# A graph attention layer: the clamp of the message weights in an instruction of its own, with its result in PSUM

## The chip, the core and the metric

One core of a Trainium2 chip runs the whole kernel in one launch. The metric is the device time in microseconds. The kernel before takes 2019.45 us, the median of three runs (2014.69 to 2023.74). Five engines run side by side, each through its own list of instructions in order: TensorE (PE, with its weight loads PEld), VectorE (DVE), ScalarE (ACT), GpSimd (POOL) and SyncE (SP). They wait for each other through semaphores.

## The reference, cut to what matters

A graph has 6250 nodes of 64 features and 206250 edges, sorted by destination. Each edge makes four scores, one for each head of 16 features, and the exponential of a clipped score weighs the value of the edge's source node. The sums go to the destination nodes, the input is added, and a layer norm over 64 features ends it.

```python
Qh = (x @ Wq.T + bq).reshape(n, H, D)          # n 6250, H 4, D 16
Kh = (x @ Wk.T + bk).reshape(n, H, D)
Vh = (x @ Wv.T + bv).reshape(n, H, D)
Ee = (edge_attr @ We.T + be).reshape(-1, H, D) # 206250 edges
score = (Kh[src] * Qh[dst] * (1.0 / np.sqrt(D)) * Ee).sum(-1)
score = jnp.exp(jnp.clip(score, -5.0, 5.0))
msg = Vh[src] * score[..., None]
wV = jax.ops.segment_sum(msg, dst, num_segments=n)
x = _layernorm(x + wV.reshape(n, H * D), axis=-1)
```

## The kernel before, in words

**Tiles and groups.** The edges are cut into 1612 tiles of 128 edges, one edge to a partition, and eight tiles make a group `g`; there are 202 groups. Two groups make a step `s`, apart from the last eight groups, which are steps of their own. After a stage that makes a table of keys and values in HBM (`kv_tab`) and a table of queries, one Python loop over `g` (L1014) writes out the instructions of all groups by hand. No scheduler reorders them: the order of the calls in that loop is the order on each engine.

**What one turn of the loop does.** POOL fetches the keys and values of the sources, 128 rows to an indirect DMA (`gather_kv`, L296), into one of five tiles `kv` in SBUF; most groups need eight of these DMAs, some need six because PE makes the rows of their last two tiles itself. PE turns the edge features and the queries of a group into `room` and `qq` in PSUM; ACT adds a bias (`eb`, L755), DVE multiplies the two (`term`, L769) and PE transposes the result into `qe` (L775), one of two PSUM banks that alternate by group. From there the group goes through DVE and ACT:

- `products` (L806, L808), DVE: `prod` is the keys of `kv` in SBUF times `qe` in PSUM, and `score` its sum over each head, 128 x 32.
- `weigh` (L813, L815), ACT: the upper clip and the exponential, into `weight`, a tile of 128 x 32 in SBUF.
- `message` (L830), DVE: one SCALAR_TENSOR_TENSOR instruction takes the larger of `weight` and the constant `LEAST` (e to the power of -5, the lower clip) and multiplies it with the values of `kv`. Both of its tensors lie in SBUF. Its output overwrites `qe`, except in the last steps, where it goes into `kv`.
- `keep` (L844), ACT, copies that to `msg` rounded, and `take` (L850), DVE, stores what the rounding left. PE adds the messages of a step up by one-hot matrices into `room` in the next turn (`sums`).

**What shares these engines.** PE also makes rows of `kv` by one-hot products, in batches `m` over pieces of the node table: DVE writes one-hot matrices (`hots`, L696, named `hot`, or `thin` where ACT widens them at L707), PE multiplies them (`picks`, into the two banks `pick`), DVE selects from the two banks (`picked`, L722 and L723, into `x`), and PE makes the rows from that (`picked_kv`, into `qq`). DVE also adds the sums of a step to a ring (`add`, L900 to L909), once in two turns; that work is called the ring's adds below. L744 is the line of a helper that records nearly all matmuls of the loop.

**The order around the change.** Within a turn DVE runs the products, the next group's `term`, the ring's adds if there are any, the first one-hot matrix of the next turn, `message`, the other one-hot matrices, `onehot_edges` (L792) at the end of a step, `take`, and `picked` where a batch ends.

**The bank of constants.** `still` (L660) is one PSUM bank of 128 x 512 f32 that holds what DVE reads again and again: `col` and `block2`, from which the one-hot matrices are compared, and `sum_`, into which the ring's adds reduce.

Of the kernel before, what the change touches and what calls it, by code (L numbers as in the profile page):

```python
# [14 lines left out]
OP = mybir.AluOpType  # L15
AX = mybir.AxisListType

P = 128
N = 6250
C = 64  # L20
H = 4
D = C // H
E = 206250
T = -(-E // P)
G = 8
# [31 lines left out]
LEAST = math.exp(-CLIP)  # L57
# [57 lines left out]
def place_of(g):  # L115

    s = max(s for s in range(NS) if STEPS[s][0] <= g)
    return s, (g - STEPS[s][0]) * G
# [31 lines left out]
def tile_gnn(ctx: ExitStack, tc: tile.TileContext, x, x_blocks, by_rows, xT, wT, bias, beT, weT, eT, src, src_rows,  # L150
             dst, dst_rows, out):
    nc = tc.nc
# [16 lines left out]
    def kv_of(g):  # L169

        s = max(s for s in range(NS) if STEPS[s][0] <= g)
        j = (g - STEPS[s][0]) * G
        return kvs[s % KVB][:, j:j + G, :]
# [479 lines left out]
    with tc.If(rv == 0) as branch:  # L653

        with tc.tile_pool(name="work", bufs=2) as work, \
# [3 lines left out]
            OH, OF, EB, TERM, MSG, SCORE, WEIGHT, HOT = ({} for _ in range(8))  # L659
            still = fixed.tile([P, 4 * P], F32, name="still")  # L660
# [7 lines left out]
            pa = room[:, 1, :2 * PA]  # L668
            folded = room[:, 1, 2 * PA:2 * PA + 2 * C].rearrange("p (b c) -> p b c", c=C)
            sum_ = still[:, 2 * P:2 * P + C]  # L670
            px = [fixed.tile([P, 4 * P], F32, name=f"pick{k}") for k in range(2)]
            xs = [accp.tile([P, 4 * P], F32, name=f"x{k}") for k in range(2)]
            qq = fixed.tile([P, G // 2, P], F32, name="qq")
# [143 lines left out]
            def message(g, lo, hi):  # L817
                s, k = place_of(g)
                n = hi - lo
                if s < WHOLE:  # L820
                    if k == 0:
                        MSG[s] = work.tile([P, 2 * G, 2, C], F32R, name="msg")
                        if s >= ONES:
                            MSG[s] = MSG[s].rearrange("p g i c -> p (g i c)").bitcast(BF16)[:, :G * 3 * C] \
                                .rearrange("p (g i c) -> p g i c", i=3, c=C)
                    to = qe[g % 2][:, lo:hi, :]
                else:
                    MSG[s] = kvs[(s - 2) % KVB][:, G:, :C]
                    to = MSG[s][:, lo:hi, :]
                nc.vector.scalar_tensor_tensor(  # L830
                    to.rearrange("p g (h d) -> p g h d", h=H),
                    WEIGHT.pop(g)[:, :, :, None].to_broadcast([P, n, H, D]), LEAST,
                    kv_of(g)[:, lo:hi, C:].rearrange("p g (h d) -> p g h d", h=H),
                    op0=OP.max, op1=OP.mult)

            def part_of(g, i):

# [176 lines left out]
            for g in range(NG + 1):  # L1014
# [46 lines left out]
                if now:  # L1061
                    message(g, *some_of(g)[0])
                for lo, hi in some_of(g)[1:] if now else []:
                    products(g, lo, hi)
                    weigh(g, lo, hi)
                    message(g, lo, hi)
# [255 lines left out]
```

## Time and profile before

| what | value |
|---|---|
| median of the runs | 2019.45 us |
| lowest and highest run | 2014.69 and 2023.74 us |
| the profiled execution's own time | 2023.01 us |
| its span, first to last instruction | 2021.2 us |
| granted TensorE clock, mean | 0.939 |
| PE busy | 1723.6 us, 85% of the span |
| DVE busy | 1485.3 us, 73% |
| ACT busy | 1327.1 us, 66% |
| POOL busy | 1256.9 us, 62% |

A busy time adds up an engine's instructions; what is left of the span is waiting. DVE instructions that don't wait for each other overlap by some tens of ns, so two rows can cover the same moment. A row of the timeline has start, duration, engine, line, operation and tiles, and in brackets the idle time ahead of it with what ended it. A row of the waits names who waited for whom, with total us, times and the longest. The chain of waits goes back from the last instruction, at each step to what released it; its pieces are the work that set the end.

### The profile page before, as it was taken

The page shows a single profiled execution, that of the slowest core. Times are in us where ns is not written, and L with a number is a line of the kernel's source. Part 1 is how long each engine was busy: PE and PEld are TensorE (multiplying, and loading weights), DVE is VectorE, ACT ScalarE, POOL GpSimd, SP SyncE. Part 2 cuts the span into 40 slices and gives each one's busy share as a digit, 9 for nine tenths or more (in the row PEclk, how much of TensorE's full clock was granted, in tenths as well). Part 3 has the DMA queues.
Part 4 walks back from the last instruction along what each step waited for, and adds up shares of the span by engine and source line. Part 5 has one row for each costly group of instructions (what it writes and reads, how often), then busy time and mean ns, then how long its engine had stood idle before and what let it go on. Part 6 is the DMA issues. An engine that isn't in the chain of part 4 may idle for free.

```text
span 2021.2 us, 25631 instructions
## 1 busy us (share of the span) xinstructions
PE 1723.6 (85%) x7993; PEld 1249.4 (62%) x7993; DVE 1485.3 (73%) x2650; ACT 1327.1 (66%) x2047; POOL 1256.9 (62%) x1310
## 2 busy tenths in 40 slices
PE   7468989888888888979888898888888998888995
PEld 6336666666666665656666666666666666656763
DVE  5367777777777786877777777777777777677886
ACT  3356676666666666766667766666766667576774
POOL 6566666666666666666666666666666666666441
PEclk9789999999999998999999999899999999999997
DMA  6524233233233332343333332333323333333320
GB/s 178 174 72 134 87 104 109 85 110 104 86 104 106 88 103 85 104 122 90 103 101 87 107 107 83 109 95 98 103 87 115 103 89 104 99 92 109 96 80 21
DMA packets 116116, 203.70 MB, mean 101 GB/s; under 512 B 54784, under 2 KB 56425, under 8 KB 115855
## 3 DMA queue, kind: packets, MB, share of 16 engines
q1 hardware_dynamic: 73932, 116.94, 18.7%
q0 software_dynamic: 41600, 83.97, 14.7%
q10 hardware_dynamic: 436, 1.04, 0.2%
q8 instruction: 65, 1.06, 0.2%
q14 instruction: 83, 0.68, 0.1%
HBM read 194.25 MB, written 7.59 MB: 100 GB/s over the span
## 4 chain that ended last, share of the span: by engine, by line
PE 60%; DVE 18%; issue 8%; ACT 6%; another core or an unknown queue 5%; DMA 2%; POOL 1%; SPq 0%; DVEq 0%; ACTq 0%; POOLq 0%
PE pick L744 35%; PE room L744 10%; PE qq L744 9%; PE qe L775 4%; DVE hot L696 4%; DVE score L808 2%; DVE qe L830 2%; DVE prod L806 1%; DVE term L769 1%; DVE msg L850 1%; DVE thin L696 1%; DMA kv<-kv_tab,src_i 1%; PE ps L513 1%; DVE x L722 1%
## 5 line engine op out<-in xcount | busy, mean ns | idle before, releaser
L296 POOL DMA_INDIRECT kv<-kv_tab,src_i x1260 | 1216.6, 966 | 709.4 <-issue 272.9
L744 PE MATMUL pick<-hot,parts 128*128 128x512 f32 x3900 | 1133.0, 433 | 127.6 <-DVE x L722 57.4
L744 PEld LDWEIGHTS pick<-hot,parts 128*128 128x128 f32 x3900 | 737.8, 197 | 426.7 <-issue 175.6
L696 DVE TENSOR_TENSOR hot<-from,still 128x1024 fp32r<-128x1024 bf16 x231 | 280.2, 1213 | 0.2 <-ACT from L258 0.2
L707 ACT ACTIVATE hot<-thin 128x1024 fp32r<-128x1024 bf16 x234 | 245.4, 1049 | 20.6 <-remote 16.8
L755 ACT ACTIVATE eb<-room,be_col 128x512 f32<-128x512 f32 x202 | 137.1, 678 | 150.5 <-DVE y L957 57.4
L769 DVE TENSOR_TENSOR term<-eb,qq 128x512 f32<-128x512 f32 x202 | 137.3, 679 | 125.8 <-PE qq L744 101.6
L844 ACT ACTIVATE msg<-qe 128x512 fp32r<-128x512 f32 (+1 forms) x206 | 123.2, 598 | 161.4 <-DVE qe L830 65.8
L744 PE MATMUL room<-et,we_sb 128*128 128x512 f32 x404 | 224.5, 638 | 4.3 <-ACT eb L755 3.6
L813 ACT ACTIVATE score<-score,five_p 128x32 f32<-128x32 f32 x203 | 64.2, 316 | 249.4 <-DVE score L808 161.5
L279 ACT ACTIVATE to<-to,one_p 126x1024 bf16<-126x1024 bf16 x198 | 225.7, 1140 | 0.1
L273 ACT ACTIVATE to<-kb,minus_row 126x1024 bf16<-126x1024 uint8 x198 | 225.2, 1137 | 0.0
L775 PE MATMUL qe<-ident,term 128*128 128x128 f32 x806 | 134.2, 292 | 61.1 <-DVE term L769 38.7
L775 PEld LDWEIGHTS qe<-ident,term 128*128 128x128 f32 x806 | 103.1, 150 | 114.1 <-DVE term L769 55.1
L722 DVE SCALAR_TENSOR_TENSOR x<-odd,upper,pick 128x512 f32<-128x512 int32 x77 | 57.3, 744 | 153.9 <-PE pick L744 84.8
L744 PE MATMUL qq<-w,x 128*128 128x128 f32 x1248 | 163.2, 285 | 5.3 <-issue 4.1
L806 DVE TENSOR_TENSOR prod<-kv,qe 128x512 f32<-128x512 f32 x203 | 136.9, 674 | 37.0 <-issue 13.7
L830 DVE SCALAR_TENSOR_TENSOR qe<-weight,kv 128x512 f32<-128x512 f32 x200 | 140.2, 701 | 30.2 <-ACT weight L815 20.6
L744 PEld LDWEIGHTS qq<-w,x 128*128 128x128 f32 x1248 | 153.6, 200 | 14.0 <-issue 8.1
L696 DVE TENSOR_TENSOR thin<-from,still 128x1024 bf16<-128x1024 bf16 x231 | 157.0, 680 | 0.0
L808 DVE TENSOR_REDUCE score<-prod 128x32 f32<-128x512 f32 x203 | 138.5, 682 | 7.0
L850 DVE TENSOR_TENSOR msg<-qe,msg 128x512 fp32r<-128x512 f32 x194 | 132.1, 681 | 4.3 <-ACT msg L844 2.7
(166 smaller groups left out, 1486.7 us busy)
## 6 DMA issues: line engine op xcount, KB each, us to landing
et<-in_eT SPq DMA_DIRECT2D x100, 512.0 KB
kb<-key_tab SPq DMA_DIRECT2D x101, 252.0 KB
kv<-kv_tab,src_i POOLq DMA_INDIRECT x1260
srcs<-in_src_rows SPq DMA_DIRECT2D x78, 256.0 KB
qw<-q_tab SPq DMA_DIRECT2D x202, 15.8 KB
kv_tab<-kv_sb SPq DMA_DIRECT2D x4, 640.0 KB
q_tab<-q SPq DMA_DIRECT2D x5, 480.0 KB
out<-y SPq DMA_DIRECT2D x2, 512.0 KB
```

The costliest lines, as they stand in the source:

```text
L273: nc.scalar.activation(TO[g][:, :n, :], KB.pop(g)[:, :n * P].rearrange("p (j e) -> p j e", j=n), AF.Square, bias=minus_row3[:3 * W])
L279: nc.scalar.activation(TO[g][:, :n, :], TO[g][:, :n, :], AF.Relu, bias=one_p[:3 * W], scale=-1.0)
L296: return nc.gpsimd.indirect_dma_start(out=kv_of(g)[:, j, :], out_offset=None, in_=kv_tab[:, :], in_offset=bass.IndirectOffsetOnAxis(ap=src ...
L696: nc.vector.tensor_tensor(to.rearrange("p b (a c) -> p b a c", c=2), pairs((FROM if hi < UNITS else OVER)[m])[:, None].to_broadcast(shape) ...
L707: nc.scalar.activation(*THIN.pop(0), AF.Copy)
L744: mark.append(nc.tensor.matmul(*aps, **kw))
L769: nc.vector.tensor_mul(TERM[g][:, :n], EB.pop(g)[:, :n], qq[:, :n])
L775: nc.tensor.transpose(qe[g % 2][:, 2 * k:2 * k + 2, :], TERM[g][:, k, :], ident)
L806: nc.vector.tensor_mul(prod, kv_of(g)[:, lo:hi, :C], qe[g % 2][:, lo:hi, :])
L808: nc.vector.tensor_reduce(SCORE[g], prod.rearrange("p g (h d) -> p g h d", h=H), axis=AX.X, op=OP.add)
L830: nc.vector.scalar_tensor_tensor(to.rearrange("p g (h d) -> p g h d", h=H), WEIGHT.pop(g)[:, :, :, None].to_broadcast([P, n, H, D]), LEAST ...
L850: nc.vector.tensor_sub(part_of(g, 1)[1], left, part)
```

## The change

The lower clip is taken out of `message`'s instruction. A new TENSOR_SCALAR instruction of DVE takes the larger of `weight` and `LEAST` and writes it to `least_`, 32 columns of the bank `still` that nothing used. A TENSOR_TENSOR instruction then multiplies `least_`, read from PSUM and repeated over the 16 features of a head, with the values of `kv` in SBUF. The output and everything else stay as they were.

```diff
             sum_ = still[:, 2 * P:2 * P + C]
+            least_ = still[:, 3 * P:3 * P + G * H].rearrange("p (g h) -> p g h", h=H)
...
-                nc.vector.scalar_tensor_tensor(
+                nc.vector.tensor_scalar(least_[:, :n], WEIGHT.pop(g), LEAST, None, op0=OP.max)
+                nc.vector.tensor_tensor(
                     to.rearrange("p g (h d) -> p g h d", h=H),
-                    WEIGHT.pop(g)[:, :, :, None].to_broadcast([P, n, H, D]), LEAST,
+                    least_[:, :n, :, None].to_broadcast([P, n, H, D]),
                     kv_of(g)[:, lo:hi, C:].rearrange("p g (h d) -> p g h d", h=H),
-                    op0=OP.max, op1=OP.mult)
+                    op=OP.mult)
```

Two places of DVE's order show it. The first is the first group of the loop, without ring's adds, in the order before; `hot` and `thin` are the one-hot matrices, `y` stands for the tile whose room they borrow there, and the brackets name the engines whose semaphores an instruction waits for.

```order
L769 TENSOR_TENSOR term<-eb,qq 128x512 [waits PE_49,Activation_49]
L696 TENSOR_TENSOR hot<-y,still 128x1024
L830 SCALAR_TENSOR_TENSOR qe_762<-weight,kv_66 128x512 [waits Activation_49]
L696 TENSOR_TENSOR thin<-y,still 128x1024
L850 TENSOR_TENSOR msg<-qe_762,msg 128x8x64 [waits Activation_49]
```

The same place in the changed program, whose lines are one or two further down:

```order
L770 TENSOR_TENSOR term<-eb,qq 128x512 [waits PE_49,Activation_49]
L697 TENSOR_TENSOR hot<-y,still 128x1024
L831 TENSOR_SCALAR still<-weight 128x32 [waits DVE_49,Activation_49]
L832 TENSOR_TENSOR qe_762<-still,kv_66 128x512 [waits DVE_49]
L697 TENSOR_TENSOR thin<-y,still 128x1024
L852 TENSOR_TENSOR msg<-qe_762,msg 128x8x64 [waits Activation_49]
```

One instruction that waited for ACT alone has become two, and both wait for DVE itself: the clamp for the one-hot matrix ahead of it, which reads the same tile `still`, and the multiply for the clamp. The second place is a turn with the ring's adds, before:

```order
L909 TENSOR_SCALAR ring<-still,below 128x64
L696 TENSOR_TENSOR hot<-from,still 128x1024
L830 SCALAR_TENSOR_TENSOR qe_763<-weight,kv_69 128x512 [waits Activation_49]
L696 TENSOR_TENSOR thin<-from,still 128x1024
L696 TENSOR_TENSOR hot<-over,still 128x512
```

And in the changed program:

```order
L911 TENSOR_SCALAR ring<-still,below 128x64
L697 TENSOR_TENSOR hot<-from,still 128x1024
L831 TENSOR_SCALAR still<-weight 128x32 [waits DVE_49,Activation_49]
L832 TENSOR_TENSOR qe_763<-still,kv_69 128x512 [waits DVE_49]
L697 TENSOR_TENSOR thin<-from,still 128x1024
```

Here too the pair stands where the one instruction stood. The other engines' orders in the loop are the same in both programs.

## The prediction

> **What bounds the kernel now.** I read the page first, then the chain of waits, then who waits for whom on PE and DVE. The page gives the busy times and the chain by engine; the table of windows gives the loop alone, the stretch from 100 to 1950 us (columns: window, length, then busy us and instructions of PE, PEld, DVE, ACT, POOL, the granted clock, DMA share, GB/s).
>
> ```profile
> PE 60%; DVE 18%; issue 8%; ACT 6%; another core or an unknown queue 5%; DMA 2%; POOL 1%; SPq 0%; DVEq 0%; ACTq 0%; POOLq 0%
> 100.00:1950.00 1850.00, 1617.57 (x7578) 1169.92 (x7576) 1390.26 (x2387) 1252.21 (x1880) 1175.73 (x1218) 0.95 0.33 99
> ```
>
> In the loop PE is busy 1618 of 1850 us (87%) and DVE 1390 (75%). PE leads and holds 60% of the chain; DVE is second with 18%. DVE has 460 us without work in the loop, 2.3 us for each of its some 200 messages. The waits (who, for whom: us, times, longest) say where that slack lies, and where PE has none against DVE:
>
> ```profile
> DVE term L769 <- PE qq L744: 101.6, 49, 4.5
> DVE x L722 <- PE pick L744: 84.8, 31, 4.8
> DVE qe L830 <- ACT weight L815: 20.6, 20, 1.4
> ```
> ```profile
> PE pick L744 <- DVE x L722: 57.4, 15, 5.9
> PE qe L775 <- DVE term L769: 38.7, 23, 10.7
> ```
>
> DVE waits for PE mostly ahead of `term` and of `x`, few times but long. PE waits for DVE for the same two, 96 us in 38 waits. So the two engines take turns in leading: a DVE that is late by some tenths of a microsecond loses nothing in the turns where it would wait next, and all of it in the turns where PE waits for it.
>
> How often the message is in such a turn is read from the chain by line, the row that carries the sum:
>
> ```profile
> by line: PE pick L744 35.1%; PE room L744 10.3%; PE qq L744 9.0%; issue 8.0%; another core or an unknown queue 4.9%; PE qe L775 3.9%; DVE hot L696 3.6%; DVE score L808 1.6%; DVE qe L830 1.5%; DVE prod L806 1.4%; DVE term L769 1.3%; DVE msg
> ```
> ```profile
> 1039.91 0.70 DVE qe L830
> ...
> 1046.04 0.61 DVE qe L830
> ```
>
> L830 holds 1.5% of 2021.2 us, 30.3 us. Its pieces on the chain (start, us) are 0.61 us where it overlaps its neighbour and 0.70 where it doesn't, so 30.3 us are about 46 pieces: 46 of 203 messages, 23%, lie on the path that sets the end.
>
> **What the change does to DVE's queue.** It removes one instruction for each message and adds two, with two waits for DVE itself. The rows of DVE's groups (line, operation, out<-in, shapes, count, busy us, mean ns, idle us) give the prices:
>
> ```profile
> L830 DVE SCALAR_TENSOR_TENSOR qe<-weight,kv 128x512 f32<-128x512 f32 x200 | 140.2, 701 | 30.2 <-ACT weight L815 20.6 <-issue 3.8 <-ACT score L813 1.4
> L806 DVE TENSOR_TENSOR prod<-kv,qe 128x512 f32<-128x512 f32 x201 | 136.3, 678 | 37.0 <-issue 13.7 <-remote 12.9 <-PE pick L744 7.6
> L852 DVE TENSOR_TENSOR qe<-qe,msg 128x512 f32<-128x512 f32 x6 | 4.2, 696 | 0.3
> L909 DVE TENSOR_SCALAR ring<-still,below 128x64 f32<-128x64 f32 x94 | 25.8, 275 | 0.0
> L446 DVE TENSOR_SCALAR bkv_all<-bkv_all 128x64 f32<-128x64 f32 x1 | 0.2, 184 | 0.0
> L409 DVE TENSOR_SCALAR three<-three_i 128x42 f32<-128x42 int32 x1 | 0.2, 177 | 0.0
> L460 DVE TENSOR_SCALAR most<-most 112x2 f32<-112x2 f32 x1 | 0.2, 169 | 0.0
> L900 DVE TENSOR_REDUCE still<-room 64x64 f32<-64x128 f32 x194 | 57.9, 299 | 83.5 <-PE pick L744 29.8 <-PE qq L744 15.3 <-remote 12.9
> ```
>
> *The multiply.* A TENSOR_TENSOR with one input in PSUM and one in SBUF takes 678 ns (L806, output in SBUF) to 696 (L852, output in PSUM like the new one). The old one took 701. The saving is 5 to 23 ns; I take 0.02 us.
>
> *The clamp.* No instruction of before reads 32 columns of SBUF and writes PSUM. TENSOR_SCALARs with constants in SBUF take 169 ns for 2 columns, 177 for 42 and 184 for 64; with PSUM as source and a per-partition factor 64 columns take 275. The bounds are 0.169 and 0.275 us; I take 0.18, by the 42 columns. [...]
>
> *The waits.* The timeline of DVE shows what a wait of DVE for itself costs (start, us):
>
> ```profile
> 1038.67 1.21 DVE L696 TENSOR_TENSOR hot<-from,still 128x1024 fp32r<-128x1024 bf16 x1
> 1039.91 0.70 DVE L830 SCALAR_TENSOR_TENSOR qe<-weight,kv 128x512 f32<-128x512 f32 x1
> 1040.52 0.68 DVE L696 TENSOR_TENSOR thin<-from,still 128x1024 bf16<-128x1024 bf16 x1
> ...
> 1042.91 0.68 DVE L806 TENSOR_TENSOR prod<-kv,qe 128x512 f32<-128x512 f32 x1
> 1043.63 0.69 DVE L808 TENSOR_REDUCE score<-prod 128x32 f32<-128x512 f32 x1
> ...
> 1044.83 1.21 DVE L696 TENSOR_TENSOR hot<-from,still 128x1024 fp32r<-128x1024 bf16 x1
> 1045.96 0.69 DVE L830 SCALAR_TENSOR_TENSOR qe<-weight,kv 128x512 f32<-128x512 f32 x1
> 1046.56 0.68 DVE L696 TENSOR_TENSOR thin<-from,still 128x1024 bf16<-128x1024 bf16 x1
> ```
>
> L808 waits for L806 and starts 0.04 us after its end (1043.63 against 1042.91 + 0.68). Without such a wait an instruction starts 0.08 us before the end of the one ahead: L830 at 1045.96, 1.13 us after a matrix that takes 1.21. But in the first group of rows, a turn with the ring's adds, L830 starts 0.03 us after the matrix's end although it waits for ACT alone, as if it waited for DVE. [...] The sum needs the two rows only.
>
> The clamp has two waits, for the matrix and for ACT. Of two waits one may take an instruction of its own in the queue. The chain shows such at `prod`, which waits for many DMAs:
>
> ```profile
> 1041.34 0.05 issue
> 1041.39 0.05 DVEq L806
> 1041.44 0.05 issue
> 1041.48 0.05 DVEq L806
> ```
>
> One is 0.10 us with its issue. The gap ahead of the clamp is then between 0.03 and 0.10 us; I take 0.06. The multiply follows 0.03 after the clamp, and what comes next overlaps it by 0.08.
>
> *The sum for one message*, from the start of the matrix ahead to the start of the one behind. Before: 1.85 us with the ring's adds (1038.67 to 1040.52), 1.73 without (1044.83 to 1046.56). After, either way: 1.21 + 0.06 + 0.18 + 0.03 + 0.68 - 0.08 = 2.08 us. That adds 0.23 us with the ring's adds and 0.35 without. L900 stands twice in each of them, 194 / 2 = 97 messages have them and 106 don't: 0.29 us in the mean, 59 us over 203 messages. The lower bounds (0.169, 0.03) give 0.25, the upper ones (0.275, 0.10, 0.696) 0.44.
>
> *What is queued behind.* DVE's next one-hot matrices, `of`, `take` and the selection `x` all start that much later; so do ACT's `keep`, which waits for the message, and PE's next picks and sums behind those. 77% of the messages have DVE's own idle time as cover; if that cover is gone, the rest of the 59 us comes on top.
>
> *The sum for the kernel.* 46 x 0.29 = 13 us on the path of before. A message 0.29 us longer also brings on the path some that ended just ahead of it; I take 26% in place of 23%, so 53 x 0.29 = 15 us. PE's matmuls, ACT, SP's transfers and the order of POOL's gathers are unchanged.
>
> *What it takes away.* The old instruction reads two tensors from SBUF, the new ones one each. POOL shows that this matters to the gathers (first the group's min/median/max and count, then the page's mean, then four in a row around the message at 1039.91):
>
> ```profile
> L296 POOL DMA_INDIRECT kv<-kv_tab,src_i x1260: 939/947/1470, 64.4 to 1985.1; - x180
> ```
> ```profile
> L296 POOL DMA_INDIRECT kv<-kv_tab,src_i x1260 | 1216.6, 966 | 709.4 <-issue 272.9
> ```
> ```profile
> 1039.09 0.94 POOL L296 DMA_INDIRECT kv<-kv_tab,src_i  x1 [0.30 <-issue]
> 1040.34 1.08 POOL L296 DMA_INDIRECT kv<-kv_tab,src_i  x1 [0.30 <-issue]
> 1041.73 0.95 POOL L296 DMA_INDIRECT kv<-kv_tab,src_i  x1 [0.30 <-PE pick L744]
> 1042.98 0.95 POOL L296 DMA_INDIRECT kv<-kv_tab,src_i  x1 [0.31 <-issue]
> ```
>
> The gather that starts inside the message (1039.91 to 1040.61) takes 1.08 us, its neighbours 0.94 and 0.95. The mean lies 19 ns above the median; over 1260 gathers that is 24 us of POOL's time, all of which I expect to go. On the path it is worth little: POOL holds 1% of the chain, so the 2% that gathers get shorter is 0.4 us.
>
> Against the profiled execution's own span that is 2021.2 + 15 = 2036 us. It was timed at 2023.01, 3.6 us above the median of the runs, and the same 15 us on 2019.45 give 2034.5; I forecast 2035 us. Half a percent, 10 us, is about what a measurement of this kernel can tell from no change.
>
> **The rivals.**
> - *The slack takes it (2020 to 2029 us).* DVE idles 2.3 us for each message, eight times what is added, and ACT has slack too. For it: most waits of DVE end with PE. Against it: 46 messages are on the chain, and nothing else on it gets shorter. With half of the 46 absorbed by paths that are nearly as long it is 7 us, 2026.
> - *The gathers were what held it (2005 us).* [...] As a mechanism here: shorter gathers land earlier, `prod` starts earlier, and the 24 us return, less what DVE adds on its own path; faster by 24 - 10 = 14 us if POOL paces the loop. That decides only where DVE waits for gathered rows. The 2% of DMA and 1% of POOL in the chain, and POOL's own waits for PE's marks (in the last rows), speak against it.
> - *DVE becomes the bound (2050 to 2080 us).* If most of the messages' 0.29 us is felt, because ACT's `keep` and PE's picks fall behind in each turn, the time rises by up to 59 us, by 90 with the upper bound.
> - *The change doesn't free POOL.* Gathers stay at 966 ns; the time differs by the 0.4 us above.
>
> **How the numbers follow.** The forecast, 8 to 30 us more, gets 60%; the slack 24%; DVE as the bound 9%; the gathers 7%. The last rival changes no number and is within the first. The range leaves out the gathers, the lowest part of the slack, and the part of the third rival above 2057: 2021 to 2057. Slower by over 0.5% means above 2029.5: most of the forecast and all of the third rival, 65%. Within 0.5%: the slack and the forecast's low end, 28%. Faster: 7%.
>
> **What would show it.** In the profile after, the clamp should be 203 rows of 0.17 to 0.28 us, 0.03 to 0.10 us behind a matrix's end; the multiply should be 0.68 to 0.70 us and 0.03 us behind the clamp; DVE should be busier by 203 x (0.18 - 0.02) = 32 us; the mean of the gathers should be at the median, 947 ns; DVE's share of the chain should rise, and its idle time ahead of `term` and `x` shrink. I am wrong if DVE's rows are as said and the time stays (then its slack is deeper than the chain shows), or if the gathers get shorter and `prod` no longer waits while the time falls.

## The result, and the profile after

The change makes the kernel slower by a third of a percent: 2026.98 us against 2020.08 (medians of 12 runs each), ratio 1.0032, 95% interval 1.0019 to 1.0045. That is 6.5 us (3.8 to 9.1): here and below the microseconds of a change are its ratio times the time before, which need not be the difference of the medians (6.9 us here). The direction is the forecast one. The size is less than half of the 15 us that were forecast.

The page after, busy times and chain by engine:

```profile
PE 1728.4 (85%) x7993; PEld 1251.6 (62%) x7993; DVE 1527.8 (75%) x2853; ACT 1327.5 (66%) x2047; POOL 1232.9 (61%) x1310
PE 56%; DVE 19%; issue 11%; ACT 6%; DMA 2%; another core or an unknown queue 2%; POOL 2%; DVEq 0%; SPq 0%; ACTq 0%; POOLq 0%
```

DVE has 42.5 us more work (1527.8 against 1485.3; 32 were forecast), POOL has 24.0 us less (1232.9 against 1256.9), and the profiled execution's span grew by 5.2 us (2026.4 against 2021.2). The groups of DVE after show the price of the new pair, and those of the gathers what went away:

```profile
L832 DVE TENSOR_TENSOR qe<-still,kv 128x512 f32<-128x512 f32 x200 | 139.9, 699 | 7.2 <-DVE still L831 0.4
L831 DVE TENSOR_SCALAR still<-weight 128x32 f32<-128x32 f32 x201 | 39.1, 195 | 44.0 <-ACT weight L816 19.3 <-ACT score L814 5.9 <-issue 0.3
```
```profile
L296 POOL DMA_INDIRECT kv<-kv_tab,src_i x1260 | 1193.6, 947 | 737.2 <-issue 283.4
```

The clamp takes 195 ns, the multiply 699, as long as the instruction that it replaces (701). The mean of the gathers is 947 ns, at their median, as forecast. Gather by gather the traces say the same: before, the 243 gathers that overlapped a message took 1043 ns in the mean and the others 947; after, the 232 that overlapped the multiply took 946. The timeline of DVE after shows the waits, first a turn with the ring's adds, then one without:

```profile
1043.10 1.21 DVE L697 TENSOR_TENSOR hot<-from,still 128x1024 fp32r<-128x1024 bf16 x1
1044.42 0.19 DVE L831 TENSOR_SCALAR still<-weight 128x32 f32<-128x32 f32 x1
1044.65 0.70 DVE L832 TENSOR_TENSOR qe<-still,kv 128x512 f32<-128x512 f32 x1
1045.26 0.68 DVE L697 TENSOR_TENSOR thin<-from,still 128x1024 bf16<-128x1024 bf16 x1
...
1049.56 1.21 DVE L697 TENSOR_TENSOR hot<-from,still 128x1024 fp32r<-128x1024 bf16 x1
1050.88 0.19 DVE L831 TENSOR_SCALAR still<-weight 128x32 f32<-128x32 f32 x1
1051.11 0.70 DVE L832 TENSOR_TENSOR qe<-still,kv 128x512 f32<-128x512 f32 x1
1051.71 0.68 DVE L697 TENSOR_TENSOR thin<-from,still 128x1024 bf16<-128x1024 bf16 x1
```

The clamp starts 0.11 us behind the end of the matrix (1044.42 against 1043.10 + 1.21). From matrix to matrix it is 2.16 and 2.15 us, where before it was 1.85 and 1.73. Over the 203 rows of before it is alike: the 94 messages with the last of the ring's adds (L909) among DVE's work since the message before start 0.02 to 0.04 us behind the end of the instruction ahead, and 73 of the other 109 start 0.05 to 0.09 us ahead of it; what holds the 94 back is not shown. So a message costs DVE 0.31 us more with the ring's adds and 0.42 without; by the forecast's counts of 97 and 106 that is 0.37 us in the mean and 75 us over 203 messages. That is an upper figure: 29 messages of before start over 0.2 us after the end of DVE's instruction ahead, most of them waiting for ACT's weight, and such a message loses only 0.23 us (the second stretch below shows one). With these it is about 69 us. Either way DVE's queue got longer by more than the 59 us that were forecast, and the kernel by 6.5. The question is where the other 60 us and more went.

### One stretch that cost nothing, and one that cost all

The chain of waits answers it where the same stretch can be read in both traces. This is the chain before around the two messages that the prediction quoted, from the ring's adds to `x` (start, us; lines between left out):

```profile
1037.61 0.30 DVE still L900
...
1048.37 0.60 DVE msg L850
1048.97 4.84 another core or an unknown queue
1053.81 0.75 DVE x L722
```

The same stretch in the chain after:

```profile
1042.04 0.30 DVE still L902
...
1053.52 0.60 DVE msg L852
1054.12 4.11 another core or an unknown queue
1058.24 0.75 DVE x L723
```

DVE's work up to `msg` became 0.72 us longer (11.48 us from 1042.04 to 1053.52, against 10.76 from 1037.61 to 1048.37), two messages of 0.31 and 0.42. The piece behind it became 0.73 us shorter. From the ring's adds to `x` it is 16.20 us in both. The piece of the "unknown queue" is time in which DVE had nothing to do; the timeline before says the same (rows of DVE, then the next rows of POOL and of PE):

```profile
1048.29 0.68 DVE L850 TENSOR_TENSOR msg<-qe,msg 128x512 fp32r<-128x512 f32 x1
1053.80 0.75 DVE L722 SCALAR_TENSOR_TENSOR x<-odd,upper,pick 128x512 f32<-128x512 int32 x1 [4.83 <-remote]
1053.91 0.95 POOL L296 DMA_INDIRECT kv<-kv_tab,src_i  x1 [2.48 <-remote]
1054.60 0.73 PE L744 MATMUL pick<-hot,parts 128*128 128x512 f32 x2 [4.30 <-DVE x L722]
```

DVE was idle for 4.83 us ahead of `x`, and `x` reads what PE's picks made. The profile does not name who released it, so the chain steps back to the instruction before it on DVE and counts DVE's work as the path. POOL has no row for 2.48 us up to nearly the same moment, and PE none for 4.30; what held them all is not shown. In this stretch the added 0.72 us went into DVE's idle time, so the messages were not on the path here.

The other kind is a stretch in which DVE has no such idle time. The chain before and after, from ACT's weight through two messages to PE's transposes:

```profile
1943.09 0.33 ACT weight L815
...
1956.95 0.66 PE qe L775 x4
```
```profile
1946.13 0.33 ACT weight L816
...
1960.52 0.66 PE qe L776 x4
```

It is 13.86 us before and 14.39 after, 0.53 us more. The first message here waits for ACT, so it loses the clamp, its wait and nothing ahead of it, 0.23 us, and the second, with the ring's adds, 0.31: 0.54. All of it is felt up to there.

I then went through the chain of before piece by piece. Of its 46 messages, 21 have DVE work behind them that ends in a piece of the unknown queue of 0.8 us or more (2.9 to 6.6 in all but two places) before the chain leaves DVE. The other 25 have no such piece and are taken to be like the second stretch; only the two stretches above were compared in both traces. 25 x 0.37 = 9.3 us. The count is one execution's: by the same rule the chain of the changed kernel has 41 messages and 9 ahead of such pieces in the profile after, 43 and 19 in that of e1, so 32 and 24 are left.

### The profile page after: what moved, and what is told of

Its sections match the earlier page's. It is cut to its first block, busy times and chain, and to the rows that moved or that the text cites. A ratio compares the mean times of both kernels' runs of the same rounds, so it can differ in the third digit from the quotient of the medians.

```text
span 2026.4 us, 26036 instructions
## 1 busy us (share of the span) xinstructions
PE 1728.4 (85%) x7993; PEld 1251.6 (62%) x7993; DVE 1527.8 (75%) x2853; ACT 1327.5 (66%) x2047; POOL 1232.9 (61%) x1310
## 4 chain that ended last, share of the span: by engine, by line
PE 56%; DVE 19%; issue 11%; ACT 6%; DMA 2%; another core or an unknown queue 2%; POOL 2%; DVEq 0%; SPq 0%; ACTq 0%; POOLq 0%
PE pick L745 33%; PE room L745 10%; PE qq L745 9%; PE qe L776 4%; DVE hot L697 3%; POOL kv L296 2%; DVE score L809 2%; DMA kv<-kv_tab,src_i 2%; DVE prod L807 2%; DVE term L770 2%; DVE qe L832 1%; DVE x L724 1%; ACT to L273 1%; DVE msg L852 1%
## 5 line engine op out<-in xcount | busy, mean ns | idle before, releaser
L296 POOL DMA_INDIRECT kv<-kv_tab,src_i x1260 | 1193.6, 947 | 737.2 <-issue 283.4
L807 DVE TENSOR_TENSOR prod<-kv,qe 128x512 f32<-128x512 f32 x203 | 137.1, 676 | 33.4 <-remote 23.8
L832 DVE TENSOR_TENSOR qe<-still,kv 128x512 f32<-128x512 f32 x200 | 139.9, 699 | 7.2 <-DVE still L831 0.4
L723 DVE SCALAR_TENSOR_TENSOR x<-odd,upper,pick 128x512 f32<-128x512 int32 x77 | 57.3, 744 | 115.4 <-PE pick L745 79.3
```

Source lines behind the costliest of these rows:

```text
L296: return nc.gpsimd.indirect_dma_start(out=kv_of(g)[:, j, :], out_offset=None, in_=kv_tab[:, :], in_offset=bass.IndirectOffsetOnAxis(ap=src ...
L807: nc.vector.tensor_mul(prod, kv_of(g)[:, lo:hi, :C], qe[g % 2][:, lo:hi, :])
L832: nc.vector.tensor_tensor(to.rearrange("p g (h d) -> p g h d", h=H), least_[:, :n, :, None].to_broadcast([P, n, H, D]), kv_of(g)[:, lo:hi, ...
```

## The experiments

The runs came in three sets, e, f and g, in each of which all kernels and the kernel before ran on one chip; there the kernel before takes 2005.17, 2004.23 and 2004.57 us. The theories' names are those of the expectations. Theory A says that the chain's share is felt and that the shorter gathers give it back. Theory B says that the gathers give nothing and that less is felt; theory N is its sharper form, with the 25 messages. Theory O keeps the prediction's 46. Theory U takes all turns as alike, and theory K gives more to the turns that follow the end of a batch, called turns behind a batch below.

**The change again.**

> The changed kernel itself, beside the others on one chip. Its profile gave a clamp of 195 ns, 106 ns behind the matrix ahead, and a multiply of 699 ns, 34 ns behind the clamp: 2.16 us from matrix to matrix in place of 1.73 or 1.85, 0.37 us more per message, 75 us of DVE's queue. Both theories: ratio to before 1.002 to 1.0045, gathers at a mean of 947 ns.

Measured: 2013.01 us, ratio 1.0050 (1.0032 to 1.0068), 10 us; gathers at 945 ns. The ratio is just above what was expected; its interval overlaps that of the first measurement.

**The clamp into SBUF, with the same wait.** The multiply reads two tensors from SBUF again. `behind` adds a wait for its second argument, and `HOTS[-1]` is the one-hot matrix ahead. The lines taken out are the changed kernel's.

```diff
+                least_ = work.tile([P, G, H], F32, name="least_")
-                nc.vector.tensor_scalar(least_[:, :n], WEIGHT.pop(g), LEAST, None, op0=OP.max)
+                behind(nc.vector.tensor_scalar(least_[:, :n], WEIGHT.pop(g), LEAST, None, op0=OP.max), HOTS[-1])
```

> The clamp writes a tile of SBUF, and waits for the matrix ahead as in the changed kernel, so DVE's queue has nearly the same cost and the multiply reads two tensors from SBUF as before. Theory A (the added time is felt on 23% of the messages, 17 us, and the shorter gathers give some 10 us back): the return is gone, 2036 us, ratio 1.006 to 1.010, gathers at a mean of 966 ns again. Theory B (the message's share of the chain overstates what is felt; the gathers give nothing): the ratio stays at 1.002 to 1.0045 although the gathers are long again.

Measured: 2018.35 us, ratio 1.0066 (1.0050 to 1.0083); the gathers' mean was 970 ns. That is in theory A's range and above theory B's; but here the change itself, at 1.0050, is above B's range too, and the two intervals overlap. Undecided.

**The same without the wait for the matrix.** As above, without `behind`.

> As the run before, without the wait of the clamp for the matrix: about 0.21 us more per message than before the change, 43 us of DVE's queue. Theory A: 46 messages of 0.21 us, 10 us, ratio 1.004 to 1.006. Theory B: 43/75 of what the change costs, 4 us, ratio 1.001 to 1.003.

Measured: 2012.80 us, ratio 1.0040 (1.0023 to 1.0057). The interval overlaps both theories' ranges. Undecided.

**A constant in PSUM instead of the weights.** This measures the gathers' part by itself. It leaves out the multiplication by the weights; `WEIGHT` holds ACT's instruction here, so that the wait for it stays.

```diff
+            least_ = still[:, 3 * P:3 * P + G * H].rearrange("p (g h) -> p g h", h=H)
+            nc.vector.memset(still[:, 3 * P:3 * P + G * H], 1.0)
...
-                nc.vector.scalar_tensor_tensor(
+                ins = nc.vector.scalar_tensor_tensor(
...
-                    WEIGHT.pop(g)[:, :, :, None].to_broadcast([P, n, H, D]), LEAST,
+                    least_[:, :n, :, None].to_broadcast([P, n, H, D]), LEAST,
...
+                behind(ins, WEIGHT.pop(g))
```

> It leaves out the weights: the one instruction of before stays, with its wait for ACT's weight, but reads the constant 1 from the bank of constants instead of the weight in SBUF. No instruction and no wait of DVE is added; only the second SBUF input is gone, and the gathers should have a mean of 947 ns. Theory A: about 10 us faster than before, ratio 0.994 to 0.996. Theory B: ratio 0.999 to 1.001.

Measured: 2004.51 us, ratio 0.9998 (0.9984 to 1.0013). The gathers did get shorter:

```profile
L296 POOL DMA_INDIRECT kv<-kv_tab,src_i x1260 | 1195.1, 949 | 717.1 <-issue 274.5
```

POOL had 1195.1 us of gathers, 21.5 us less than the 1216.6 before, and the time did not move. Theory A falls: by the interval at most some 3 us can come back this way.

**More work where DVE idles ahead of `x`.**

```diff
                 if g in READY:
+                    nc.vector.memset(work.tile([P, 4 * P], F32, name="spare", bufs=1), 0.0)
                     picked(READY.index(g))
```

> The kernel before, with a memset of 128 x 512 f32 on DVE ahead of the selection x in the 78 turns that end a batch, about 0.5 us of DVE's queue each, nothing else. In the chain of before, 19 stretches of DVE work lead from a message to x. Theory O (all 46 messages of the chain lie on the path): 19 x 0.5 us, about 10 us, ratio 1.004 to 1.006. Theory N (where the chain has a piece of an unknown queue between DVE's work and x, DVE was idle there and had that much slack; 13 of the 19 are such): 6 x 0.5 us, 3 us, ratio 1.000 to 1.003.

Measured: 2007.35 us, ratio 1.0026 (1.0013 to 1.0039), 5 us. The groups of DVE in this run:

```profile
L1126 DVE MEMSET spare<- 128x512 f32 x78 | 37.8, 485 | 4.4
L722 DVE SCALAR_TENSOR_TENSOR x<-odd,upper,pick 128x512 f32<-128x512 int32 x77 | 54.5, 708 | 127.5 <-PE pick L744 64.5 <-remote 36.2 <-issue 19.2
```

The memset is 485 ns and in this run's rows starts 0.05 to 0.06 us behind the end of the `msg` ahead of it (1012.45 against 1011.72 + 0.68); how closely `x` follows it where DVE doesn't idle is not shown. From these rows I estimate about 0.5 us in the queue, as I had said. The ratio is in the range put down for theory N and below theory O's; in microseconds, 5 lies between theory N's 3 and theory O's 10. Most of the 78 x 0.5 = 39 us that were added was not felt. DVE's idle time ahead of `x` is 127.5 us in this run, where before it was 84.8 + 48.2 + 20.9 = 153.9 in the waits for PE, for a remote releaser and for issue. That fits, but two profiles of the changed kernel (after and e1) differ there too, 115.4 and 134.2 us, so the 26 us alone would not show where the work went.

**The clamp twice.**

```diff
-                nc.vector.tensor_scalar(least_[:, :n], WEIGHT.pop(g), LEAST, None, op0=OP.max)
+                weight = WEIGHT.pop(g)
+                for _ in range(2):
+                    nc.vector.tensor_scalar(least_[:, :n], weight, LEAST, None, op0=OP.max)
```

> The changed kernel with the clamp done twice, one behind the other: 0.23 us more per message, 0.60 us against before. Theory O (46 messages on the path): 46 x 0.60 = 28 us, ratio 1.013 or more. Theory N (25 on the path): 25 x 0.60 = 15 us and some that come on the path, ratio 1.006 to 1.010.

Measured: 2020.67 us, ratio 1.0081 (1.0057 to 1.0106), 16 us. Theory N has it; theory O's 28 us lies outside the interval.

**The clamp five times, in two sets of turns.** `range(5 if g - 1 in READY else 1)`, and the reverse. `READY` lists the turns that end a batch, so the first run has the five clamps in the 78 turns behind a batch.

> The changed kernel with the clamp done five times in the 78 turns that follow the end of a batch, and once in all others: 0.92 us more in each of those turns, 72 us of DVE's queue beyond the change. 4 of the chain's messages are in such turns. Theories O and N: 4 x 0.92 = 4 us beyond the change, ratio 1.005 to 1.008. Theory U (any turn counts alike, a tenth of all of DVE's added time is felt): 7 us beyond the change, ratio 1.007 to 1.009.

Measured: 2035.26 us, ratio 1.0158 (1.0136 to 1.0180), 32 us. All three theories miss: 72 us in the turns behind a batch cost some 22 us beyond the change's 10, where 4 to 7 were expected. The waits of PE in this run, with those of before (33.7 us in 21 waits for the same releaser, ACT's `kv`) in the second fence:

```profile
PE qq L745 <- ACT kv L740: 71.7, 49, 2.7
```
```profile
PE qq L744 <- ACT kv L739: 33.7, 21, 3.0
```

In such a turn ACT places the two tiles that PE made (`kv`, L740 here) behind `keep` in its queue, `keep` waits for the message, and PE's queries of the next but one group write into the bank that ACT must empty first. By that order a message that comes 1.3 us late holds PE up. That this path had a short slack before is an inference: only 4 of the chain's 46 messages are in such turns. But the same row tells apart the kernels with one clamp in these turns and those without. The four lines are from after, e1, g1 and, with the clamp in the other turns alone, g2:

```profile
PE qq L745 <- ACT kv L740: 42.1, 29, 2.5
PE qq L745 <- ACT kv L740: 39.3, 30, 2.2
PE qq L745 <- ACT kv L740: 41.5, 28, 2.0
PE qq L745 <- ACT kv L740: 32.8, 19, 3.0
```

Without a clamp it is 33.7 us before and 32.7 to 33.4 in e4, f1 and g3; with the clamp in SBUF it is 39.9 in e2 and 35.7 in e3, which adds less to the queue. So the change itself adds 6 to 8 us to PE's waits on this path, and nothing where these turns are left as they were. How much of that reaches the end is not shown.

> The changed kernel with the clamp done five times in all turns but those 78: 125 messages, 0.92 us more each, 115 us of DVE's queue beyond the change. Theory O (42 of the chain's messages are there): 39 us beyond the change's 17, ratio 1.025 or more. Theory N (21 of them): 19 us beyond the change's 8 and some that come on the path, ratio 1.013 to 1.020. Theory U: 12 us beyond the change, ratio 1.009 to 1.011.

Measured: 2034.20 us, ratio 1.0151 (1.0128 to 1.0173), 30 us. Theory N has it, theories O and U don't.

**The change in one set of turns alone.** The pair behind `if g - 1 in READY` with the old instruction in the `else`, and the reverse.

> The change in the 78 turns that follow the end of a batch alone; the others keep the one instruction of before. 29 us of DVE's queue. Theory N (the chain of before counts what is felt; 4 of its messages are in such turns): 4 x 0.37 = 1.5 us, ratio 0.9995 to 1.002. Theory K (in these turns ACT's placing of kv stands behind the message in ACT's queue and PE waits for it, so they bear more than the chain shows; the run with five clamps gave 24 us for 72): a third of 29 us, 10 us, ratio 1.003 to 1.006.

Measured: 2009.53 us, ratio 1.0022 (1.0009 to 1.0036), 4 us.

> The change in all turns but those 78: 125 messages, 46 us of DVE's queue. Theory N: 21 x 0.37 = 8 us, ratio 1.003 to 1.005. Theory K: what is left of the change's 7 to 10 us, about none, ratio 0.999 to 1.002.

Measured: 2010.58 us, ratio 1.0019 (0.9997 to 1.0041), 4 us. The two sum to 8 us, between the 6.5 and the 10 of the whole change. Neither theory N's split (1.5 and 8 us) nor theory K's (10 and none) is met: g1's ratio lies between the two, g2's at the upper end of theory K's. By the ratios the 78 turns behind a batch bear about as much as the 125 others, but the intervals (1.8 to 7.2 us, and -0.6 to 8.2) are too wide to decide it.

**The wait alone.**

```diff
-                nc.vector.scalar_tensor_tensor(
+                ins = nc.vector.scalar_tensor_tensor(
...
+                behind(ins, HOTS[-1])
```

> The kernel before, with its one instruction made to wait for the matrix ahead of it on DVE, as the clamp does in the changed kernel; nothing else. It should start 0.106 us behind the matrix in place of 0.03 behind or 0.08 ahead of its end: 0.07 us more with the ring's adds and 0.19 without, 27 us of DVE's queue. Theory N: 25 x 0.13 = 3 us, ratio 1.000 to 1.003.

Measured: 2005.55 us, ratio 1.0008 (0.9993 to 1.0023). The old instruction starts 0.12 us behind the matrix, as the clamp does:

```profile
1005.98 1.21 DVE L696 TENSOR_TENSOR hot<-from,still 128x1024 fp32r<-128x1024 bf16 x1
1007.31 0.70 DVE L830 SCALAR_TENSOR_TENSOR qe<-weight,kv 128x512 f32<-128x512 f32 x1
```

The wait by itself costs 1.6 us by the ratio, within what was expected and not clear of zero.

## Why the prediction was wrong

- **That it gets slower, by DVE's queue and not by the gathers: right.** The pair stands where the order showed it, and each of its waits does too.
- **The price of a message: too small.** The clamp was taken at 0.18 us and is 0.195; the multiply at 0.68 and is 0.70, so it saves nothing; the gap ahead of the clamp was taken at 0.06 and is 0.11, just above the upper bound of 0.10. 0.37 us came out in place of 0.29. By itself this would have made the forecast larger: 53 x 0.37 = 20 us.
- **"46 of 203 messages, 23%, lie on the path that sets the end": the step that failed.** The row of the chain was read as work that sets the end, and nearly half of it stands ahead of idle time of the same engine. Both rows that the prediction quoted for it, at 1039.91 and 1046.04, are messages of the stretch above in which nothing was felt. 21 of the 46 stand ahead of idle time of DVE that the chain prints as an unknown queue. The 5% of such pieces was in the row of the chain that carried the sum, and I did not ask what stood behind them. The 25 others give 9.3 us, just above the interval of the first measurement (3.8 to 9.1 us) and within that of e1 (6.4 to 13.6). The longer clamps speak for the smaller number: f2 measured 16 us where the 46 give 28, f4 30 where they give 56. The count by turns is not confirmed: in f3 and g1 the turns behind a batch cost more than the 4 messages that the chain has there. So it is in part luck that 25 x 0.37 comes near the total; shown is that the 46 are too many, not that it is these 25.
- **The 26% in place of 23% for messages that come on the path: the right kind of term, lost in the wrong base.** f3 shows such a path at a longer delay, the way through ACT's `kv`, and PE's 6 to 8 us of added waits there show it for the change itself.
- **The gathers lose their 24 us and the time loses 0.4: right on the first, and 0.4 lies within e4's interval.** With one SBUF input in the message in place of two their mean of 966 ns fell to 947 (949 in e4), and with two again (e2) it was 970.
- **The rival of the slack** (2020 to 2029 us, 24%) describes what happened better than the forecast did; its own worked case, half of the 46 absorbed, is nearly the count of 21. The prediction's own sign of being wrong, slack deeper than the chain shows, is what came.

What stays open is which turns the 6.5 us of the change itself come from, since 4 us for each set is hardly clear of the spread, and what ends the idle time that the chain prints as an unknown queue.

## What to carry to other kernels

A share of the chain is not yet what is felt. Follow each of its stretches to the piece behind it: where an engine's work on the chain ends in an unknown piece, read that engine's own idle time at the same moment, and if it idled there, its work may have had that much to spare. The stretches without such a gap are the better count for a price in an engine's queue, but no bound: in f3 more work in turns that had 4 messages on the chain cost over 20 us, and PE's waits for ACT's `kv`, a path that had hardly shown before, rose by 38 us. The same stretch in two traces, from one named instruction to another, shows at once whether an added cost was felt in it. And busy time that goes on an engine that waits for others' marks need not come back: POOL lost 21.5 us of it in e4, and the time stayed within 3 us.

## What was not expected of the hardware

- An instruction that waited for DVE and for ACT started 0.11 us behind the end of the one-hot matrix ahead of it in nearly every turn where ACT was done (0.10 to 0.12 us for 172 of the 203 clamps of after); with one wait for DVE alone the gap was 0.04 us (the multiply behind the clamp, 1044.65 against 1044.42 + 0.19).
- A TENSOR_TENSOR that reads PSUM and writes PSUM took 699 ns for 128 x 512 (the multiply), one that writes SBUF 678 (`prod`); with its first input read from PSUM the old form of instruction took 697 ns (e4) in place of 701.
